# Banded attention beside two routed expert layers: the band's place, the pace of the chains, and the row buffers

## The chip, the cores and the metric

The kernel runs on one core of one Trainium2 chip. The metric is the device time of one execution in microseconds (us). In the text PE is the engine of the matrix products (TensorE), PEld its weight loads, DVE the vector engine, ACT the scalar engine, POOL the GpSimd engine, SP the engine that issues most of the transfers. SBUF is the on-chip memory, PSUM the memory that PE writes its products to.

## The reference

Four batches of 512 rows, each row 128 wide, go through four stages, each followed by a residual sum and a layer norm:

1. attention with 16 heads of width 8, in which row t sees only the rows from t-64 to t+64 (the band): `scores = where(valid, q.k / sqrt(8), -inf)`, softmax over the band, times v, then an output product;
2. a first expert layer: a dense gated block for all rows, and 12 experts of which each row takes two;
3. a state-space layer;
4. a second expert layer: 8 experts of which each row takes two, each with a layer norm of its own.

## The kernel before

**Attention** (`attention`, L858) is one loop over steps. There are eight steps to a batch (`steps = 2 * NT`): four blocks of 128 rows times two halves of the heads. At step g the loop emits, in this order:

- `attention_exp` for step g (L775): PE multiplies q and k for eight heads (the products `pse`, L787, four PSUM banks), ACT takes the exponential into `pt` (L791), POOL zeroes what lies outside the band (L795);
- `attention_max` for step g+9 (L742): the maximum score of each row and head, which is later folded into q so that the exponential does not overflow. For each of four banks (two heads each) PE first writes the band (0 inside, -1e30 outside) into the bank as a product of the identity with a bfloat16 tile (L752), then adds the scores of two heads (`psc`, L758); DVE then takes the maximum of both heads with one `tensor_reduce` per bank (L764);
- `attention_values` for step g-2 (L800): PE multiplies the exponentials with v (L810);
- parts of the next batch's q, k, v (`attention_qk`, `attention_v`);
- `advance(2)` (L906): the next two pieces of every chain that is open.

The loop runs from g = -9 to g = 33. So nine steps hold maxima alone, the steps 0 to 22 hold maxima and exponentials, and the steps 23 to 33 hold no maxima.

**A chain** belongs to a batch b and opens at g = 8b + 9, after that batch's last `attention_values`. It is a Python generator: `attention_out` (L819: scaling by the sums, the product `po` with the output weights, the layer norm) and then `moe0_shared` (L910: the gates, the routing, which ends in eight scatters of rows into a table in DRAM on POOL's queue, L454 and L460, and beside it the dense block). It has 21 `yield`s; each `next` emits one piece, and the 22nd `next` ends it. What is left of the chains after the loop is emitted behind it, one chain after the other, before the expert tiles.

PSUM has a pool of six banks for all of these products (`bank`, L61), handed out in turn: a step of attention takes four for `pse` and four for `psc`.

**The expert layers** (`tiles`, L574) run over 43 and then 39 tiles of 128 rows. In round t, in this order: the loads of tile t+3 (`route_load`, L527: SP issues the rows into a tile `io` and then the expert's weights into `wt`; POOL copies a bias), the transpose of tile t+1 on PE (`pxs`, L548), the up products of tile t with their activations, and the down product of tile t-1, whose result DVE writes into the same `io`; POOL then scatters it from there to DRAM (`ys`, L460). So an `io` buffer is held from the load of its tile until that tile's scatter has been read out. There are six `io` buffers (L534) and four `wt` buffers. In the second layer POOL also adds a bias row into `io` (L1545), copies the bias of tile t+3 (L539) once DVE has used that of tile t-1 (L1563), and DVE takes statistics (L1560 to L1566).

**The order** on each engine is the order in which the Python code emits (`as_written`, L76): every engine runs its instructions in that order, scatters alone may pass one another. Nothing is reordered by a scheduler inside this part.

Of the kernel before, what the change touches and what calls it, by code (L numbers as in the profile page):

```python
# [9 lines left out]
F32 = mybir.dt.float32  # L10
BF16 = mybir.dt.bfloat16
I32 = mybir.dt.int32
AF = mybir.ActivationFunctionType
ALU = mybir.AluOpType
AX = mybir.AxisListType

P = 128
# [3 lines left out]
D = 128  # L21
# [11 lines left out]
NEG = -1.0e30  # L33
# [6 lines left out]
class Kernel:  # L40
# [91 lines left out]
    def consts(self):  # L132
        nc, c = self.nc, self.const

        def t(shape, name):
            return c.tile(shape, F32, tag=name, name=name)

        self.ident = t([P, P], "ident")
        make_identity(nc, self.ident)

        def filled(value, name, shape=(P, 1)):
            x = t(list(shape), name)
            nc.gpsimd.memset(x, value)
            return x

        self.eps5 = filled(1e-5, "eps5")
        self.eps6 = filled(1e-6, "eps6")
        self.half_pi = filled(math.pi / 2, "half_pi")

        self.ident_bf = c.tile([P, P], BF16, tag="ident_bf", name="ident_bf")  # L150
        nc.vector.tensor_copy(self.ident_bf, self.ident)
        self.band = c.tile([P, 256], BF16, tag="band", name="band")
        nc.gpsimd.memset(self.band, 0.0)
        nc.gpsimd.affine_select(
            out=self.band, in_=self.band, compare_op=ALU.is_ge, fill=NEG,
            base=0, pattern=[[1, 256]], channel_multiplier=-1,
        )
        nc.gpsimd.affine_select(
            out=self.band, in_=self.band, compare_op=ALU.is_ge, fill=NEG,
            base=2 * HALF, pattern=[[-1, 256]], channel_multiplier=1,  # L160
        )

        self.rev = t([P, 16], "rev")
        for e in range(16):
            nc.gpsimd.memset(self.rev[:, e : e + 1], float(16 - e))


        self.ones_bf = c.tile([P, P], BF16, tag="ones_bf", name="ones_bf")
        nc.gpsimd.memset(self.ones_bf, 1.0)
        self.before = c.tile([P, P], BF16, tag="before", name="before")  # L170
        nc.gpsimd.affine_select(
            out=self.before, in_=self.ones_bf, compare_op=ALU.is_gt, fill=0.0,
            base=0, pattern=[[1, P]], channel_multiplier=-1,
        )
        self.one_row = filled(1.0, "one_row", (P, 16))
        self.zero = filled(0.0, "zero", (P, ROW))
        number = c.tile([P, 64], I32, tag="number", name="number")
        nc.gpsimd.iota(number, pattern=[[1, 64]], base=0, channel_multiplier=0)
        self.tile_no = t([P, 64], "tile_no")
        nc.vector.tensor_copy(self.tile_no, number)  # L180
        self.first_row = t([P, 16], "first_row")
        nc.vector.tensor_scalar(self.first_row, self.tile_no[:, :16], float(NB * T), None, ALU.mult)

        place = c.tile([P, NB * NT], I32, tag="place", name="place")
        nc.gpsimd.iota(place, pattern=[[2 * P, NB * NT]], base=0, channel_multiplier=2)
        self.place = t([P, NB * NT], "place_f")
        nc.gpsimd.tensor_copy(self.place, place)
        dump = c.tile([P, 48], I32, tag="dump", name="dump")
        nc.gpsimd.iota(dump, pattern=[[P, 48]], base=0, channel_multiplier=1)
        self.dump = t([P, 48], "dump_f")  # L190
        nc.gpsimd.tensor_copy(self.dump, dump)
# [335 lines left out]
    def route_load(self, r, t, up, w, biases):  # L527

        nc = self.nc
        self.route_regs(r, t)  # L530
        reg = r["reg"]
        wt = self.wt.tile([P, 6 * D], F32, tag="wt", name=f"wt_{r['name']}{t}")[:, :w]
        bias = self.wt.tile([P, U1], F32, tag="bias", name=f"bias_{r['name']}{t}")[:, : r["bias"]]
        io = self.wt.tile([P, 3 * D + 4], F32, tag="io", name=f"io_{r['name']}{t}", bufs=6)  # L534
        nc.sync.dma_start(out=io[:, :ROW], in_=r["table"][bass.ds(reg[t, 0], P), :])
        nc.sync.dma_start(
            out=wt, in_=up[bass.ds(reg[t, 1], 1)].rearrange("o p w -> (o p) w")
        )
        nc.gpsimd.tensor_copy(bias, biases[:, bass.ds(reg[t, 3], r["bias"])])  # L539
        return {  # L540
            "wt": wt, "bias": bias, "row": io[:, :ROW], "xs": io[:, :D], "xt": io[:, ROW : ROW + D],
            "ys": io[:, ROW + D : ROW + 2 * D + 1],
        }
# [198 lines left out]
    def attention_max(self, b, u, s):  # L742

        nc = self.nc
        j, odd = divmod(u, 2)
        lo, hi = self.reach(j)
        w, off = hi - lo, lo - (j * P - HALF)
        banks = [
            self.bank(f"psc{b}_{u}_{i}").rearrange("p (c s) -> p c s", c=2)[:, :, :w] for i in range(4)
        ]  # L750
        for pp in banks:
            nc.tensor.matmul(  # L752
                pp, lhsT=self.ident_bf, rhs=self.band[:, None, off : off + w].to_broadcast([P, 2, w]),
                start=True, stop=False,
            )
        for i, pp in enumerate(banks):
            strip = slice(32 * i, 32 * i + 32)
            nc.tensor.matmul(  # L758
                pp, lhsT=s["q"][strip, odd, j * P : (j + 1) * P],
                rhs=s["k"][strip, odd::2, lo:hi], start=False, stop=True,  # L760
            )
        for i, pp in enumerate(banks):
            at = 32 * i + self.MAX_ROW[odd]
            nc.vector.tensor_reduce(self.maxima[b % 2][:, j, at : at + 2], pp, AX.X, ALU.max)  # L764

    def attention_max_end(self, b, s):
        nc = self.nc
# [90 lines left out]
    def attention(self, x, behind):  # L858

        self.attention_consts()
        steps = 2 * NT
        ahead, lag = steps + 1, 2
        state = [{} for _ in range(NB)]
        chains = []

        def chain(b):
            y = yield from self.attention_out(b, state[b])
            yield from behind(b, y)  # L870

        def advance(n):
            for c in list(chains):
                for _ in range(n):
                    if next(c, None) is None:
                        chains.remove(c)
                        break

        for _ in self.attention_qk(0, x[0], state[0]):
            pass  # L880
        self.attention_zeros()
        for g in range(-ahead, NB * steps + lag):
            b, u = divmod(g, steps)
            if 0 <= b < NB:
                self.attention_exp(b, u, state[b])
            b, u = divmod(g + ahead, steps)
            if u == 0 and 0 < b <= NB:
                self.attention_max_end(b - 1, state[b - 1])
            if b < NB:
                self.attention_max(b, u, state[b])  # L890
            b, u = divmod(g - lag, steps)
            if 0 <= b < NB:
                self.attention_values(b, u, state[b])
                if u == steps - 1:
                    chains.append(chain(b))
            if g == -ahead:
                self.attention_weights()
            b, u = divmod(g + ahead + 4, steps)
            if 0 < b < NB and u < 3:
                if u == 0:  # L900
                    state[b]["qk"] = self.attention_qk(b, x[b], state[b])
                next(state[b]["qk"])
            b, u = divmod(g + steps - 3, steps)
            if u == 0 and b < NB:
                self.attention_v(b, state[b])
            advance(2)  # L906
        return (part for c in chains for part in c)


# [788 lines left out]
```

## Time and profile before

| | us |
|---|---|
| median of 5 runs (826.05 to 832.53) | 829.85 |
| the profiled execution, its whole time | 826.89 |
| its span in the profile | 825.2 |

| engine, share of the span busy | |
|---|---|
| PE | 547.3 us, 66% |
| DVE | 426.7 us, 52% |
| POOL | 369.5 us, 45% |
| ACT | 310.0 us, 38% |

By stage, in time from the start of the span: weights arrive and the first maxima wait for them until about 34; maxima alone until 60.7; attention with maxima until about 201; attention without maxima until 264; the rest of the chains until 313; tiles of the first expert layer until 430; the state-space layer until 675; tiles of the second expert layer until about 786; combining and output until 825.

How to read it: a row of a timeline gives the start, the duration, the engine, the line, the operation, what it writes and reads, and how many instructions were merged (x4); in brackets stands how long the engine had been idle before it, and what ended that. A row of waits gives the waiting engine and line, what it waited for, the total, the number of times and the longest. PEclk is the granted clock of TensorE as a share of full speed.

### The profile page before, as it was taken

How to read it: one execution, taken by the hardware profiler on the slowest of the kernel's cores; microseconds unless marked ns; L12 is line 12 of the kernel's file. 1: busy time of each engine (PE TensorE's matmuls, PEld its weight loads, DVE VectorE, ACT ScalarE, POOL GpSimd, SP SyncE). 2: the span in 40 equal slices, each digit the busy share in tenths (PEclk: the TensorE clock that was granted, in tenths of full speed). 3: DMA queues.
4: the chain of work that ended last, by engine and by line, in shares of the span. 5: the costliest groups of instructions: out<-in, count | busy, mean ns of one | idle time of the engine just before them, and what ended most of it. 6: DMA issues, size and time to landing. Idle time of an engine off the chain costs nothing.

```text
span 825.2 us, 12715 instructions
## 1 busy us (share of the span) xinstructions
PE 547.3 (66%) x3912; PEld 383.1 (46%) x3912; DVE 426.7 (52%) x1384; ACT 310.0 (38%) x787; POOL 369.5 (45%) x515
## 2 busy tenths in 40 slices
PE   4389997899859356888863365656766428787700
PEld 1035452454535335887861143433544328676700
DVE  2375573576414243555543587595554335665645
ACT  2014445425644113444432547033131205455503
POOL 8103352274563342444442434366354445666641
PEclk8599997899966677999995758575575558999955
DMA  7999999960000005676747011111110124555431
GB/s 157 206 149 148 149 147 148 151 97 7 8 20 7 19 27 168 205 207 185 211 131 202 0 54 51 38 48 44 45 33 20 33 74 129 144 155 143 130 109 51
DMA packets 93933, 83.58 MB, mean 101 GB/s; under 512 B 8869, under 2 KB 78650, under 8 KB 93866
## 3 DMA queue, kind: packets, MB, share of 16 engines
q1 hardware_dynamic: 88554, 71.85, 43.6%
q0 software_dynamic: 5312, 10.92, 4.4%
q8 instruction: 32, 0.52, 0.3%
q14 instruction: 35, 0.29, 0.1%
HBM read 50.54 MB, written 32.20 MB: 100 GB/s over the span
## 4 chain that ended last, share of the span: by engine, by line
PE 38%; DVE 18%; DMA 13%; issue 11%; ACT 9%; POOL 8%; SPq 2%; POOLq 1%; ACTq 0%; DVEq 0%
DMA io_b<-table_b 4%; PE pse L787 4%; PE psc L758 4%; ACT pt L791 3%; PE pc L810 3%; POOL ys_a L460 3%; PE psc L752 2%; DMA io_a<-table_a 2%; PE py L1398 2%; PE tp_xt L284 2%; PE ph L1550 2%; DVE m L1348 2%; PE ppj L1085 2%; PE py L1394 2%; DVE y L1014 2%
## 5 line engine op out<-in xcount | busy, mean ns | idle before, releaser
L795 POOL TENSOR_SCALAR_AFFINE_SELECT pt<-pt 128x1024 f32<-128x1024 f32 (+1 forms) x64 | 61.6, 985 | 133.8 <-ACT pt L791 130.2
L764 DVE TENSOR_REDUCE maxima<-psc 128x2 f32<-128x384 f32 (+1 forms) x128 | 71.0, 617 | 59.3 <-PE psc L758 53.8
L791 ACT ACTIVATE pt<-pse 128x384 f32<-128x384 f32 (+1 forms) x128 | 59.8, 550 | 74.0 <-PE pse L787 73.9
L460 POOL DMA_INDIRECT ys_a<-io_a,at_a x43 | 42.1, 980 | 59.4 <-DVE at_a L559 52.6
L995 DVE SCALAR_TENSOR_TENSOR act<-pa,bias_a,ge 128x128 f32<-128x128 f32 x129 | 37.3, 345 | 57.7 <-ACT ge L994 35.4
L752 PE MATMUL psc<-band,ident_bf 128*128 128x384 bf16 (+1 forms) x128 | 40.2, 382 | 30.2 <-DVE maxima L764 19.6
L1553 ACT ACTIVATE hid<-ph,bias_b 128x128 f32<-128x128 f32 x156 | 44.6, 369 | 25.2 <-PE ph L1550 17.5
L787 PE MATMUL pse<-q,k 32*128 32x256 f32 (+1 forms) x512 | 48.8, 401 | 0.5 <-ACT pt L791 0.4
L460 POOL DMA_INDIRECT table_b<-r,put x32 | 32.2, 1007 | 33.9 <-DVE e_cnt L447 15.4
L994 ACT ACTIVATE ge<-pg,bias_a 128x128 f32<-128x128 f32 x129 | 38.1, 366 | 21.3 <-DVE at_a L559 7.5
L1550 PE MATMUL ph<-io_b,wt_b 128*128 128x128 f32 x312 | 43.2, 283 | 0.0
L460 POOL DMA_INDIRECT ys_b<-io_b,at_b x39 | 39.1, 1003 | 8.3 <-issue 5.7
L787 PEld LDWEIGHTS pse<-q,k 32*128 32x128 f32 x512 | 35.5, 201 | 14.4 <-issue 8.0
L568 PE MATMUL py_b<-down,hid 128*128 x312 | 42.1, 279 | 0.0
L460 POOL DMA_INDIRECT table_a<-x,put x32 | 32.5, 1016 | 19.9 <-issue 13.8
L1367 POOL TENSOR_TENSOR m<-m,gg 128x512 f32<-128x512 f32 x16 | 26.2, 1661 | 31.2 <-DVE m L1348 31.2
L1550 PEld LDWEIGHTS ph<-io_b,wt_b 128*128 128x128 f32 x312 | 39.5, 198 | 0.0
L568 PEld LDWEIGHTS py_b<-down,hid 128*128 128x128 f32 x312 | 38.7, 195 | 0.2 <-ACT hid L1553 0.2
L292 ACT ACTIVATE rstd<-mv,eps 128x4 f32<-128x4 f32 x16 | 4.7, 297 | 88.3 <-DVE mv L312 79.3
L758 PE MATMUL psc<-k,q 32*128 32x384 f32 (+1 forms) x256 | 37.0, 651 | 0.9 <-ACT k L719 0.9
L986 PE MATMUL pg<-io_a,wt_a 128*128 128x128 f32 x258 | 36.7, 279 | 0.0
L986 PE MATMUL pa<-io_a,wt_a 128*128 128x128 f32 x258 | 36.5, 278 | 0.0
(340 smaller groups left out, 1279.4 us busy)
## 6 DMA issues: line engine op xcount, KB each, us to landing
wt_a<-in_We_dram SPq DMA_DIRECT2D x43, 384.0 KB
table_a<-zero SPq DMA_DIRECT2D x12, 1040.0 KB
wt_b<-in_w_dram SPq DMA_DIRECT2D x39, 256.0 KB
table_b<-zero SPq DMA_DIRECT2D x8, 1040.0 KB
dbc<-rows SPq DMA_DIRECT2D x8, 512.0 KB
io_a<-table_a SPq DMA_DIRECT2D x43, 65.0 KB
io_b<-table_b SPq DMA_DIRECT2D x39, 65.0 KB
down<-in_We_dram SPq DMA_DIRECT2D x12, 192.0 KB
```

The lines of the kernel that those rows point to most:

```text
L460: put = self.nc.gpsimd.indirect_dma_start(out=out, out_offset=bass.IndirectOffsetOnAxis(ap=at, axis=0), in_=x, in_offset=None)
L568: nc.tensor.matmul(py[:, :D], lhsT=hidden[:, c * P : (c + 1) * P], rhs=flat[:, bass.ds(r["reg"][t, 2] + c * D, D)], start=c == 0, stop=c = ...
L752: nc.tensor.matmul(pp, lhsT=self.ident_bf, rhs=self.band[:, None, off : off + w].to_broadcast([P, 2, w]), start=True, stop=False,)
L758: nc.tensor.matmul(pp, lhsT=s["q"][strip, odd, j * P : (j + 1) * P], rhs=s["k"][strip, odd::2, lo:hi], start=False, stop=True,)
L764: nc.vector.tensor_reduce(self.maxima[b % 2][:, j, at : at + 2], pp, AX.X, ALU.max)
L787: nc.tensor.matmul(pp[:, c], lhsT=s["k"][strip, 2 * cp + c, m * P : (m + 1) * P], rhs=s["q"][strip, c, lo:hi], start=True, stop=True, skip ...
L791: nc.scalar.activation(pt[:, 2 * i : 2 * i + 2, :w], pp, AF.Exp)
L795: nc.gpsimd.affine_select(out=x, in_=x, compare_op=ALU.is_ge, fill=0.0, base=HALF if m == 0 and sign > 0 else 0, pattern=[[0, 2 * G], [sig ...
L986: nc.tensor.matmul(p[:, c * P : (c + 1) * P], lhsT=wt[:, at : at + P], rhs=xt, start=True, stop=True,)
L994: nc.scalar.activation(ge[:, cb], pg[:, cb], AF.Gelu, bias=bias[:, 3 + c : 4 + c])
L1550: nc.tensor.matmul(ph[:, cb], lhsT=s["wt"][:, cb], rhs=s["xt"], start=True, stop=True)
L1553: nc.scalar.activation(hid[:, cb], ph[:, cb], AF.Gelu, bias=s["bias"][:, c : c + 1])
```

## The change

Four edits:

- The band is no longer written into PSUM by PE. The four products of L752 in every `attention_max` are gone, and the product of the scores opens and closes its bank alone. The bfloat16 identity and the bfloat16 band are gone; the band is a float32 tile in SBUF.
- In place of one `tensor_reduce` per bank (two heads), DVE gets one `tensor_tensor_reduce` per head: it adds the band to the scores, writes the sum into a scratch tile `in_reach` in SBUF (two buffers), and gives the maximum. In the built program each of these stands as two instructions on DVE: the main one, and a second, 128x1, that writes the maximum out.
- `advance(2)` becomes `advance(3)`.
- `io` has eight buffers where it had six.

```diff
-        self.ident_bf = c.tile([P, P], BF16, tag="ident_bf", name="ident_bf")
-        nc.vector.tensor_copy(self.ident_bf, self.ident)
-        self.band = c.tile([P, 256], BF16, tag="band", name="band")
+        self.band = t([P, 256], "band")
...
-        io = self.wt.tile([P, 3 * D + 4], F32, tag="io", name=f"io_{r['name']}{t}", bufs=6)
+        io = self.wt.tile([P, 3 * D + 4], F32, tag="io", name=f"io_{r['name']}{t}", bufs=8)
...
-        for pp in banks:
-            nc.tensor.matmul(
-                pp, lhsT=self.ident_bf, rhs=self.band[:, None, off : off + w].to_broadcast([P, 2, w]),
-                start=True, stop=False,
-            )
         for i, pp in enumerate(banks):
             strip = slice(32 * i, 32 * i + 32)
             nc.tensor.matmul(
                 pp, lhsT=s["q"][strip, odd, j * P : (j + 1) * P],
-                rhs=s["k"][strip, odd::2, lo:hi], start=False, stop=True,
+                rhs=s["k"][strip, odd::2, lo:hi], start=True, stop=True,
             )
         for i, pp in enumerate(banks):
             at = 32 * i + self.MAX_ROW[odd]
-            nc.vector.tensor_reduce(self.maxima[b % 2][:, j, at : at + 2], pp, AX.X, ALU.max)
+            for c in range(2):
+                in_reach = self.ctx.tile([P, 256], F32, tag="in_reach", name="in_reach")
+                nc.vector.tensor_tensor_reduce(
+                    in_reach[:, :w], pp[:, c], self.band[:, off : off + w], 1.0, NEG, ALU.add, ALU.max,
+                    self.maxima[b % 2][:, j, at + c : at + c + 1],
+                )
...
-            advance(2)
+            advance(3)
```

## Prediction

> **What bounds the kernel now.** I read first the busy time in the stages, then timelines inside them, then the waits of SP. Columns of the first view: stretch, its length, then busy us (and instructions) of PE, PEld, DVE, ACT, POOL, then PEclk, DMA share, GB/s.
>
> ```profile
> 34.00:60.70 26.70, 22.31 (x107) 8.20 (x107) 20.35 (x42) 3.48 (x5) 0.00 (x0) 0.82 1.26 149
> 60.70:108.50 47.80, 46.12 (x431) 23.86 (x429) 26.10 (x50) 22.48 (x46) 18.45 (x20) 1.00 1.27 149
> 108.50:200.00 91.50, 80.88 (x684) 41.26 (x684) 51.48 (x127) 44.40 (x82) 40.22 (x43) 0.93 0.95 115
> 200.00:264.00 64.00, 49.65 (x438) 31.14 (x439) 24.59 (x80) 31.20 (x59) 33.60 (x40) 0.79 0.03 11
> 264.00:313.00 49.00, 24.40 (x100) 15.87 (x98) 19.36 (x66) 8.51 (x14) 18.36 (x24) 0.72 0.06 21
> 313.00:426.00 113.00, 96.20 (x802) 91.92 (x803) 56.28 (x249) 48.75 (x170) 46.97 (x79) 0.97 0.69 200
> 675.00:780.00 105.00, 80.18 (x640) 75.26 (x641) 59.63 (x252) 53.11 (x191) 65.14 (x109) 0.95 0.53 146
> ```
>
> PE bounds attention while there are maxima (96%, then 88% busy; DVE 55%). From 200 to 313 no engine is full: chains run on their latency. The tiles are nearly PE's, with holes. Timeline of DVE and PE in a step without a chain:
>
> ```profile
> 105.58 1.11 PE L752 MATMUL psc<-band,ident_bf 128*128 128x512 bf16 x4
> 106.61 1.14 PE L758 MATMUL psc<-k,q 32*128 32x512 f32 x8
> 107.69 0.86 PE L810 MATMUL pc<-pt,v 128*32 128x192 f32 x16
> 108.47 1.77 PE L787 MATMUL pse<-q,k 32*128 32x256 f32 x16
> ```
> ```profile
> 107.77 2.48 DVE L764 TENSOR_REDUCE maxima<-psc 128x2 f32<-128x512 f32 x4 [2.17 <-PE psc L758]
> ```
>
> The band takes PE about 1.05 us of this step, and DVE sits idle 2.17 us before its four maxima. Four 684 ns reductions end in 2.48 us: one each 0.6 us.
>
> After attention, the last chain's PE work waits for POOL, whose queue first empties the scatters of the chain before:
>
> ```profile
> 274.40 0.97 POOL L460 DMA_INDIRECT table_a<-x,put  x1 [0.31 <-issue]
> 275.68 0.97 POOL L460 DMA_INDIRECT table_a<-x,put  x1 [0.30 <-issue]
> 276.68 1.27 POOL L840 TENSOR_TENSOR sum<-sum,scale 128x512 f32<-128x512 f32 x1
> ```
>
> In the tiles, PE runs one every 2.12 us until the rows are late:
>
> ```profile
> 384.16 0.27 PE L548 MATMUL pxs_a<-ident,io_a 128*128 128x128 f32 x1
> 386.27 0.27 PE L548 MATMUL pxs_a<-ident,io_a 128*128 128x128 f32 x1
> 389.17 0.33 PE L548 MATMUL pxs_a<-ident,io_a 128*128 128x128 f32 x1 [0.61 <-DMA io_a<-table_a]
> ```
>
> and SP's own waits say why they are late: the load waits until a scatter has given its buffer back.
>
> ```profile
> SPq L535 <- DMA ys_a<-io_a,at_a: 30.5, 17, 4.0
> SPq L535 <- DMA ys_b<-io_b,at_b: 30.3, 21, 3.5
> ```
>
> **Price of the new DVE work.** Per head, two instructions. The main one adds an SBUF operand to a PSUM operand and writes SBUF: the row with that shape is L1423 (128x256, 414 ns); 64 elements fewer cost (692-414)/256 x 64 = 70 ns by L850 (512 wide, 692 ns), so 345 ns at 192. Queued work overlaps by 0.07 us (684 ns against 0.62), so 0.345 and 0.275 are the low ends. The second instruction, 128x1, is not in the trace: between 0.06 (a 32x1 memset, L1258, 59 ns) and 0.16 (L559 on 128x1, 159 ns). I take 0.47 (256) and 0.40 (192), mean 0.435 us, nearest to L1423 with a short second part and some overlap. Ends: 0.37 and 0.54 in the mean. A step's eight heads take 3.5 us; its four reductions took about 2.2. So DVE gets 1.3 us more in each of 32 steps, 42 us. PE loses 1.0 us per step, about 34 us in all (128 products; 40.2 us busy by the page, which counts overlap).
>
> [...]
>
> **Part by part.**
>
> 1. Maxima alone (34 to 60.7): DVE is busy 20.35 of 26.7 us. Some 8.5 steps x 1.3 = 11 us more; its idle 6.3 us was mostly PE's band and goes. Sum **+5.5**.
>
> 2. Steps 0 to 8, no chain (47.8 us, 5.3 a step): PE falls to 5.3-1.05 = 4.2; DVE needs 3.5 + 0.6 (k, v, q: 26.1 less 9 x 2.2 = 6.3 us over 9 steps, 0.7 at most) = 4.1 to 4.2. Both full, so some loss between them; six banks for eight tiles a step leave PE no lead. I take 4.65 a step: **-6**.
>
> 3. Steps 9 to 22, with a chain (91.5 us, 6.5 a step): a chain brings DVE about 17 us (layer norm, gates, transposes; rows L828 to L970), at three pieces over eight steps 2.1 a step instead of 17/11 = 1.5. DVE: 3.5 + 0.6 + 2.1 = 6.2. PE: 6.5 - 1.05 + 0.4 (the chain's 13 us over 8 instead of 11 steps) = 5.9, plus stalls, since PE's chain pieces stand behind DVE pieces of the same step, which queue behind eight heads. I take 6.65: **+2**. Six pieces more are then done by step 22 (18 of the second chain's 22 against 12).
>
> 4. Steps 23 to 33 (200 to 264): those six are gone from steps 23 and 24, which took 17 us, 8.5 each; without product pieces some 5.5: -6. The third chain opened while the second's last scatters were queued: PE waited 6.75 us at 232 for POOL's `sum`. With three pieces 22 calls fit into eight steps, so each chain ends before the next opens (the built order on POOL shows it). But POOL's six scatters in a row, 1.28 each, now stand ahead of the next step's selects; two steps of lag cover that. I take -5. Sum **-11**.
>
> 5. Behind the loop: the last chain's `po` began 13.9 us after its `sum` copy (264.1 to 278.0). Its own path is 2.1 (transposes, reciprocals) + 0.6 + 0.7 + 1.3 and hand-overs, 5.8; two scatters may still be ahead, 7.8. **-6**; one more early piece is nothing measurable.
>
> 6. First tiles: an `io` returns 8 us after its down product (386.5 end of `py`, 387.54 scatter, 391.72 next load issued, 394.5 landed by the 2.4 to 3 us loads here). With six buffers three rounds must cover that: 2.7 us a round; the mean is 2.58 (314.65 to 422.88, 42 rounds). With eight, five rounds: 1.6, below PE's 2.12. The next limits: `wt`, four buffers, freed when the up products end, leaving over 6 us for a 384 KB load; and DMA, 69% busy at 2.58, 83% at 2.15. 42 x (2.58-2.15) = 18 us at best; PE's measured holes are 113-96 = 17, of which 4 are the start. I take **-13**.
>
> 7. Second tiles: mean 2.65 (677.4 to 778.0, 38 rounds). Where rows are there, another loop shows: L1560 at 742.87 and 745.11, 2.24 us apart, through DVE's statistics, POOL's L539 and L1545. 38 x (2.65-2.25) = 15; I take **-14**.
>
> The first 34 us, the state-space layer and the end keep their waits (weights landing; L520 on routing). One conversion (1.1 us) at the start goes under those weights.
>
> Sum: 5.5 - 6 + 2 - 11 - 6 - 13 - 14 = -42.5; 826.9 - 42.5 = 784.4. The profiled execution lies 3 us below the median of the five, so I say **786**.
>
> **Rivals.**
>
> - *DVE becomes the bound (slower).* If a head costs what L1414 takes for 128x256 (663 ns) and 0.16 more, 0.82 and at 192 0.75, a step is 6.3 us. Then part 1 is 8.5 x 4.1 - 6 = +29, part 2 (6.3+0.6-5.3) x 9 = +14, part 3 (9.0-6.5) x 14 = +35; less 17 and 27: +34, **861**. For it: most of DVE's idle is already spent in the forecast. Against: L1423 is the same shape with PSUM and takes 414. It decides from 0.64 us a head, where the 42.5 us are used up (256 heads, four fifths exposed). Chance 0.12.
> - *Three pieces stall PE.* In-order waits of chain pieces add 0.9 us to each of 14 steps and the third chain saves nothing: +11 and +10, **807**. For it: PE waited up to 7 us for such pieces with two. Chance 0.14.
> - *The rows come no earlier*, because `wt` or the DMA share binds: tiles give 7 instead of 27, **806**. Against: no PE wait for `wt` is in the trace. Chance 0.13; with the stalls of the rival before, 827, chance 0.03.
> - *Cheap heads*, 0.37: parts 1 to 3 lose 5, 5 and 8 us more, **768**. Chance 0.14.
> - The change does not do quite what it says (two instructions a head, not one); that is priced above.
>
> The forecast keeps 0.44, its own range 772 to 800. The range 762 to 828 leaves out the slower case and a little below. Faster by over 0.5% (about what a measurement of this kernel can tell from no change): 0.44 + 0.14 + 0.13 + 0.14 = 0.85, less a little for mixtures, 0.84; within it 0.04; slower 0.12.
>
> **What would show it.** No L752; the main instruction near 0.41 and 0.35 us, the second under 0.16; DVE over 80% busy from 60 to 190; PE's waits for `psc` banks now ended by DVE; POOL's L840 of the last batch no longer behind scatters; `pxs` 2.15 and 2.25 us apart with no wait for rows, SP's waits on `ys` gone. A main instruction over 0.6 us, or DVE idle behind PE's chain pieces, would make the forecast wrong.

## The result and the profile after

The changed kernel takes 826.48 us (median of 52 runs, 817.52 to 831.59) against 829.0 us (94 runs, 820.44 to 837.79): a ratio of 0.9966, 95% interval 0.9953 to 0.9979. That is faster by 0.34%, inside the half per cent that the prediction set as the bound of "no change". The prediction was 786 us. The time lies just within its range (762 to 828 us), but by no merit of its reasoning: near the upper end it had only a case in which the rows come no earlier (827 us, chance 0.03), and here they do. The profiled execution took 824.23 us, its span 822.5 (before 826.89 and 825.2).

Set side by side, the two traces show a gain and a loss that nearly cancel. The marks are the first start of an operation (for a step, of its exponentials on ACT):

| stretch | before, us | after, us | difference | predicted |
|---|---|---|---|---|
| to the first exponential (maxima alone) | 61.4 | 60.4 | -1.0 | +5.5 |
| step 0 to step 10, no chain | 48.3 | 45.1 | -3.2 | -6 |
| step 10 to step 23, a chain in nearly every step | 93.2 | 133.3 | **+40.1** | +2 |
| step 23 to the last step's exponentials | 51.5 | 56.2 | +4.7 | -11 |
| from there to the first `pxs_a` | 60.2 | 51.0 | -9.2 | -6 |
| first to last `pxs_a` | 108.2 | 91.2 | -17.0 | -13 |
| first to last `pxs_b` | 100.6 | 84.0 | -16.6 | -14 |

One execution is not the kernel: a second trace of the changed kernel (run 5 below, the fastest of its twelve, 814.53 us) has 125.0 us from step 10 to step 23. So some 8 of the 40 us change from one execution to the next.

The busy time of the changed kernel in the same stages (attention runs to 295 us now, so the stretches end later); columns as before: stretch, length, busy us and instructions of PE, PEld, DVE, ACT, POOL, then PEclk, DMA share, GB/s.

```profile
34.00:60.70 26.70, 22.83 (x88) 13.18 (x86) 23.28 (x131) 3.78 (x6) 0.00 (x0) 0.69 1.33 146
60.70:107.00 46.30, 45.87 (x402) 28.43 (x401) 32.11 (x178) 24.24 (x51) 19.93 (x21) 0.93 1.26 149
107.00:190.00 83.00, 69.20 (x431) 39.06 (x428) 37.44 (x185) 29.53 (x55) 28.02 (x32) 0.69 1.04 127
344.00:442.00 98.00, 94.19 (x816) 93.92 (x817) 57.63 (x254) 50.30 (x173) 47.95 (x82) 0.95 0.77 231
```

DVE did not fill up: 37.4 us of 83 from 107 to 190. PE's clock is what changed most there: 0.69, against 0.93 before. A busy share of PE at that clock is long products here, not much work (the 83 us hold 431 products of 0.161 us of busy time each, the 91.5 us of before held 684 of 0.118).

The heads on DVE are cheap. Timeline of DVE in the changed kernel, two heads of width 256:

```profile
102.58 0.08 DVE L759 DVE_READ_ACCUMULATOR2_ANT maxima<- 128x1 f32 x1
102.58 0.42 DVE L759 CUSTOM_DVE_ANT_0 in_reach<-psc,band 128x256 f32<-128x256 f32 x1
102.93 0.08 DVE L759 DVE_READ_ACCUMULATOR2_ANT maxima<- 128x1 f32 x1
102.93 0.42 DVE L759 CUSTOM_DVE_ANT_0 in_reach<-psc,band 128x256 f32<-128x256 f32 x1
```

One head every 0.35 us: the 0.08 us of the second instruction lie under the next head's start.

But PE did not get its 1.05 us a step back. A step without a chain, at a granted clock of 1.00, PE first, then its weight loads (PEld):

```profile
77.12 1.17 PE L785 MATMUL pse<-q,k 32*128 32x256 f32 x16
78.08 2.54 PE L751 MATMUL psc<-k,q 32*128 32x512 f32 x8
80.55 1.07 PE L808 MATMUL pc<-pt,v 128*32 128x256 f32 x16
```
```profile
79.01 0.29 PEld L751 LDWEIGHTS psc<-k,q 32*128 32x128 f32 x2 [0.42 <-ACT pt L789]
79.50 0.29 PEld L751 LDWEIGHTS psc<-k,q 32*128 32x128 f32 x2 [0.20 <-ACT pt L789]
```

The eight instructions of the scores took 1.14 us before and take 2.54 now. The second row of loads says why: the third and fourth bank are still being read by ACT's exponentials of the same step (six banks, eight tiles a step), and come free one by one, 0.5 us apart. Before, the four band products ran in just that time: from 86.55 to 88.03 us they start 0.5 us apart, the last two of them held 0.17 us each by ACT's exponentials.

In a step with a chain, PE stands. The first row is the first chain's `po` before the change, the others are from the changed kernel:

```profile
118.95 1.95 PE L845 MATMUL po<-wo,sum 128*128 128x128 f32 x16
```
```profile
107.65 0.86 PE L808 MATMUL pc<-pt,v 128*32 128x192 f32 x16
111.10 0.49 PE L843 MATMUL po<-wo,sum 128*128 128x128 f32 x2 [2.59 <-POOL sum L838]
111.86 3.31 PE L843 MATMUL po<-wo,sum 128*128 128x128 f32 x14 [0.27 <-DVE sum L838]
...
126.26 2.15 PE L751 MATMUL psc<-k,q 32*128 32x512 f32 x4 [3.23 <-ACT pt L789]
...
149.55 1.01 PE L933 MATMUL tp_gt<-ident,e_g 128*12 128x128 f32 x4 [5.67 <-DVE rh L405]
```

`po` is a chain's product, and stands in PE's queue ahead of the next step's. Before, it waited for nothing. Now it waits 2.6 us for POOL, whose scaling (L838) stands behind two selects (2.14 us together), and then takes 3.8 us at a granted clock of 0.59 (111.0 to 115.2 us). At 149.55 PE has stood 5.67 us for the chain's routing on DVE, ahead of the transposes `tp_gt` of the gates; the first chain before had no such wait. At 126 it is ACT that is late: ahead of the step's exponentials its queue holds the chain's square root and four normalisations (L290, L303), with a table load of 1.28 us on either side, and the normalisations waited for DVE. This wait is not new: before, PE stood 3.20 us for ACT in a like place (131.77 us).

The first tiles went as foreseen. Their products of rows, and SP's waits for buffers (30.5 and 30.3 us before):

```profile
386.35 0.27 PE L546 MATMUL pxs_a<-ident,io_a 128*128 128x128 f32 x1
388.47 0.27 PE L546 MATMUL pxs_a<-ident,io_a 128*128 128x128 f32 x1
```
```profile
SPq L533 <- DMA ys_b<-io_b,at_b: 22.0, 14, 3.8
...
SPq L533 <- DMA ys_a<-io_a,at_a: 12.0, 15, 1.2
```

### The profile page after: what moved, and what is told of

The parts are those of the page before. It is cut to its first block, busy times and chain, and to the rows that moved or that the text cites. A ratio compares the mean times of both kernels' runs of the same rounds, so it can differ in the third digit from the quotient of the medians.

```text
span 822.5 us, 13039 instructions
## 1 busy us (share of the span) xinstructions
PE 561.6 (68%) x3784; PEld 407.6 (50%) x3784; DVE 438.2 (53%) x1767; ACT 310.2 (38%) x788; POOL 368.2 (45%) x515
## 4 chain that ended last, share of the span: by engine, by line
PE 45%; DVE 19%; issue 11%; DMA 9%; ACT 6%; POOL 5%; SPq 3%; another core or an unknown queue 0%; POOLq 0%; ACTq 0%; DVEq 0%
PE psc L751 7%; PE pse L785 5%; DMA io_b<-table_b 4%; PE pc L808 3%; PE pg L984 2%; PE pa L984 2%; PE py L1396 2%; PE ph L1548 2%; DVE m L1346 2%; PE py_a L566 2%; PE py L1392 2%; PE po L843 2%; DVE y L1012 2%; PE py_b L566 1%; PE tp_xt L282 1%
## 5 line engine op out<-in xcount | busy, mean ns | idle before, releaser
L759 DVE CUSTOM_DVE_ANT_0 in_reach<-psc,band 128x192 f32<-128x192 f32 (+1 forms) x256 | 82.6, 386 | 43.1 <-PE psc L751 36.2
L751 PE MATMUL psc<-k,q 32*128 32x512 f32 (+1 forms) x256 | 82.6, 757 | 24.8 <-DVE maxima L759 16.3
L751 PEld LDWEIGHTS psc<-k,q 32*128 32x128 f32 x256 | 39.1, 240 | 48.8 <-issue 22.1
L458 POOL DMA_INDIRECT ys_a<-io_a,at_a x43 | 42.0, 976 | 42.6 <-DVE at_a L557 40.1
L785 PE MATMUL pse<-q,k 32*128 32x256 f32 (+1 forms) x512 | 51.1, 456 | 1.2 <-issue 1.2
L992 ACT ACTIVATE ge<-pg,bias_a 128x128 f32<-128x128 f32 x129 | 38.0, 365 | 21.3 <-DVE at_a L557 16.6
L808 PE MATMUL pc<-pt,v 128*32 128x256 f32 (+1 forms) x512 | 40.8, 441 | 0.7 <-issue 0.6
```

Source lines behind the costliest of these rows:

```text
L458: put = self.nc.gpsimd.indirect_dma_start(out=out, out_offset=bass.IndirectOffsetOnAxis(ap=at, axis=0), in_=x, in_offset=None)
L751: nc.tensor.matmul(pp, lhsT=s["q"][strip, odd, j * P : (j + 1) * P], rhs=s["k"][strip, odd::2, lo:hi], start=True, stop=True,)
L759: nc.vector.tensor_tensor_reduce(in_reach[:, :w], pp[:, c], self.band[:, off : off + w], 1.0, NEG, ALU.add, ALU.max, self.maxima[b % 2][:, ...
L785: nc.tensor.matmul(pp[:, c], lhsT=s["k"][strip, 2 * cp + c, m * P : (m + 1) * P], rhs=s["q"][strip, c, lo:hi], start=True, stop=True, skip ...
L808: nc.tensor.matmul(acc[32 * i : 32 * i + 32, lo:hi], lhsT=s["v"][:, m, 4 * i + 2 * cp + c, :], rhs=pt[:, 2 * i + c, : hi - lo], start=m == ...
L992: nc.scalar.activation(ge[:, cb], pg[:, cb], AF.Gelu, bias=bias[:, 3 + c : 4 + c])
```

## The experiments

**Theory.** The loss is made by the three pieces. A chain's pieces are issued in order with the step's own work, and each one on PE, ACT or POOL holds its whole queue until the piece before it has come through another engine (above: PE for 2.59 us ahead of `po` and 5.67 ahead of `tp_gt`). The time that a chain takes in this way belongs to the chain, not to the step: before, the eleven steps of the first chain (10 to 21) took 83.3 us, after, its eight steps (10 to 18) took 81.7. With three pieces a chain is laid over three steps fewer, and those steps must be done elsewhere. **Rivals:** the DVE heads (chain pieces on DVE stand behind sixteen more instructions); PE's clock; and, for the scores' long products, that the 32-row products no longer run side by side (before, eight of 0.64 us each in 1.14 us) for another reason than banks. Times of kernels that ran together are compared with the kernel before on the same chip; ratios compare across. Runs 1 to 8 ran on one chip, 9 to 11 on a second, 12 on a third.

**1. Eight buffers alone.** `bufs=6` to `bufs=8` for `io` in the kernel before.

> The kernel before with eight io buffers alone; band still by PE, two pieces a step. In the changed kernel the first tiles' products span 91.2 us instead of 108.2 and the second tiles' 84.0 instead of 100.6; if these 33.6 us are the buffers' alone, the time is 829 - 33 = 796 us. Nothing ahead of the first tile should move. Should the tiles have gained from later rows instead (other spacing of the work around them), it would be 805 or more.

Measured: 792.11 us, ratio 0.9575 (0.952 to 0.963). `pxs_a` span 90.1 us, `pxs_b` 84.6, the first `pxs_a` at 315.9 (314.7 before). The buffers are worth the whole 35 us, and the rest of the change has lost them again.

**2. Three pieces, band still by PE.**

```diff
-            advance(2)
+            advance(3)
```

> Eight buffers and three pieces a step, band still by PE. Pieces theory: a chain beside attention takes some 80 us whatever number of pieces a step has (83 us for eleven steps before, 82 for eight in the changed kernel), so three pieces leave three steps a chain uncovered, some 9 to 10 us each time: 796 + 25 to 30 = 821 to 826 us. Rival, the DVE heads: the chains' pieces are late because they queue behind sixteen DVE instructions a step; without those three pieces cost little: 800 us or less.

Measured: 818.72 us, 0.9895 (0.985 to 0.9941): 26.6 us more than the run before, with no DVE head in it. Steps 10 to 18 take 76.1 us. The stall is the one of the changed kernel:

```profile
117.12 3.66 PE L845 MATMUL po<-wo,sum 128*128 128x128 f32 x16 [3.18 <-POOL sum L840]
```

The time is just under the 821 to 826 us that the pieces theory gave, and far from its rival's 800.

From the first exponential to the first `pxs_a` PE does the same products in runs 1 and 2. Run 2 takes 281.9 us there and run 1 254.9: PE stands idle 74.2 us against 53.4, and is busy 207.7 against 201.5, at a granted clock of 0.80 against 0.85. So most of the 27 us are waits, and the rest are longer products.

**3. Band by DVE, eight buffers, two pieces** (the changed kernel with `advance(2)`).

> The changed kernel with two pieces a step: band by DVE, eight buffers. Pieces theory: the first ten steps keep their gain of about 4 us and the chains cover eleven steps again, so 796 - 4 to -12 = 784 to 792 us. Rival, the DVE heads: the loss of 31 us in attention stays for the most part: 815 us or more.

Measured: 789.33 us, 0.9552 (0.9506 to 0.9597). With two pieces the DVE heads are no loss; 2.8 us less than in run 1, with intervals that overlap. In its trace the first `pxs_a` comes at 313.2 instead of 315.9. The rival that the heads make the loss has fallen: this kernel and the changed one differ by the third piece alone, and that piece costs 4.1% (0.9552 against 0.9966), about 34 us. From the first exponential to the first `pxs_a` PE is idle 49.2 us here, and 65.4 and 67.8 us in the two traces of the changed kernel; it is busy 202.6 us here, and 220.2 and 208.7 us there, at a clock of 0.82 against 0.73 and 0.78. The third piece brings 16 to 19 us of waits and 6 to 18 us of longer products.

**4. The same, with the values between exponentials and maxima.**

```diff
             b, u = divmod(g, steps)
             if 0 <= b < NB:
                 self.attention_exp(b, u, state[b])
+            b, u = divmod(g - lag, steps)
+            if 0 <= b < NB:
+                self.attention_values(b, u, state[b])
...
             if b < NB:
                 self.attention_max(b, u, state[b])
-            b, u = divmod(g - lag, steps)
-            if 0 <= b < NB:
-                self.attention_values(b, u, state[b])
```

> As the run before it, with the value products put between the exponentials' products and those of the maxima in each step. Bank theory: in the changed kernel the four products of the maxima take 2.3 to 2.5 us at full clock instead of 1.14, since the third and fourth wait, each by itself, for a bank that ACT's exponential of the same step gives back, a wait that the band products filled. With 0.86 us of value products in that place they take 1.6 us or less, and a step without a chain is 0.5 to 0.8 us shorter: 8 to 15 us less than the run before it. Rival: the 32-row products have lost their side-by-side run for another reason (each opens its bank itself): they still take 2.3 us or more, and the time is within 2 us of the run before it.

Measured: 783.09 us, 0.9466 (0.943 to 0.9502). PE in two steps of this run:

```profile
103.82 0.86 PE L808 MATMUL pc<-pt,v 128*32 128x192 f32 x16
104.61 1.14 PE L751 MATMUL psc<-k,q 32*128 32x512 f32 x8
105.57 2.69 PE L785 MATMUL pse<-q,k 32*128 32x256 f32 x15
```

The scores are back at 1.14 us, so they had lost nothing but their banks: bank theory right. The wait did not vanish. It moved to the exponentials' products, 2.69 us instead of 1.17, which now wait for banks that DVE gives back (their third and fourth pair start at 106.69 and 107.38 us, 0.16 us after DVE's second and fourth head end); so 6 us were gained where 8 to 15 were expected.

**5. The changed kernel again,** as the base of the next three.

> The changed kernel as it is, beside the next three on one chip: 0.9966 of the time before, as measured already; it is the base for the run after it.

Measured: 823.79 us, 0.9974 (0.9949 to 0.9998). The profiled execution took 814.53 us, the fastest of the twelve.

**6. Three pieces, spread over the step.** `advance(1)` after the exponentials, after the maxima and at the end, in place of `advance(3)`.

> The changed kernel with its three pieces a step put one after each of the step's three groups of products (exponentials, maxima, values) instead of all at the step's end. Hand-over theory: a chain takes about 80 us because PE, in order, stands at each piece's product until the piece before it has passed through DVE, POOL or ACT (82 us / 22 pieces = 3.7 us a piece); with 0.9 to 2.4 us of products between two pieces, 1 to 1.5 us a step is covered in 24 steps: 24 to 36 us less than the changed kernel, 790 to 802 us. Rival, the amount of work: three pieces a step simply give DVE and POOL more than a step lasts; where they stand in it matters little: within 5 us of the changed kernel, 821 to 831 us.

Measured: 806.41 us, 0.9756 (0.9686 to 0.9826): 17 us less than run 5, steps 10 to 18 in 65.3 us instead of 75.9. It is the same work with the same number of pieces a step, so their place counts and not only their amount; less was regained than expected. The first `po` still waited 3.4 us for POOL, and all four together 28.1 us, where the two traces of the changed kernel have 19.8 and 20.5.

**7. Two pieces, spread,** one after the values and one at the end, on run 4.

> Eight buffers, band by DVE, value products ahead of those of the maxima, two pieces a step, one after the value products and one at the end. Hand-over theory: a piece's wait is covered by the maxima's products, about 1 us in each of 24 to 33 steps with a chain: 783 - 20 to -30 = 753 to 763 us. Rival, the amount of work: 780 to 786 us.

Measured: 795.68 us, 0.9603 (0.9542 to 0.9663): a miss, 12.6 us more than run 4. In the trace, DVE's heads once wait 10.6 us for the scores: the chain's `pys` products, 7.5 us (0.79 and 1.22 us a group, as long as in the changed kernel at a granted clock of 0.50), now stand on PE between the values and the scores. A piece in the middle of a step holds up the step's own later products. That this is the whole of the 12.6 us was not shown: 2.5 us of it lie in one step ahead of every chain (step 2 to 3, 7.1 us against 4.6); the granted clock from 61 to 110 us was 0.88 here and 0.93 in run 4.

**8. One piece a step, and the rest in turns,** on run 4.

```diff
-            advance(2)
-        return (part for c in chains for part in c)
+            advance(1)
+        def rest():
+            while chains:
+                for c in list(chains):
+                    part = next(c, None)
+                    if part is None:
+                        chains.remove(c)
+                    else:
+                        yield part
+        return rest()
```

> As the run before it, but one piece a step for each chain, and what is left of the chains behind the loop done in turns, one piece of each. Hand-over theory: each piece has a whole step to pass through the other engines, so a step costs little over its products (4.5 to 5 us): 34 steps end near 225 us instead of 252, and 42 pieces in turns take some 75 us: 765 to 778 us. If the chains' pieces do not overlap behind the loop (2.7 us each, one after another), 113 us: 808 us.

Measured: 757.63 us, 0.9158 (0.9098 to 0.9219), below the expectation. The last step's exponentials come at 218.0 us (247.8 in run 4), and the first `pxs_a` at 281.1 (308.3).

**9. One piece, the rest one chain after another.**

> As the run with one piece a step (757.6 us), but what is left of the chains behind the loop is done one chain after another, as in the kernel before. The loop should end as early (218 us there). Hand-over theory: 42 pieces one after another at some 2.7 us each (before: 22 pieces between 254 and 313 us, with nothing beside them) take 113 us instead of 63: about 800 to 808 us. Rival, that the order behind the loop does not matter: 755 to 762 us.

Measured: 777.06 us, 0.9413 (0.9364 to 0.9461), between the two expectations. The loop ends as early (220.7), but the first `pxs_a` comes at 297.9. Beside run 4 this is within the intervals: in the traces one piece a step ends the loop 27.1 us earlier, and the some 40 pieces left, one chain after another, give 16.6 of them back. Of the 22.5 us between the traces of runs 9 and 8 the turns account for 14.0 (77.1 against 63.1 us from the last step's exponentials to the first `pxs_a`); 2.5 lie in a step ahead of every chain (the granted clock from 61 to 110 us was 0.87 here and 0.93 in run 8), and some 4 in a stretch of the state-space layer that no edit touches.

**10. As run 8, with the band by PE and the old order.**

> One piece a step and the rest in turns, eight buffers, but the band by PE and the step's order as before: what the DVE heads are worth where the chains no longer hold PE. If PE's products then set the step, the band's 1.05 us counts in most of 32 steps and the time is 757.6 + 15 to 30 = 773 to 788 us. If banks, not PE, set the step (the wait that moved from the maxima's products to the exponentials', 2.1 to 2.7 us instead of 1.2), the band is nearly free: 757.6 + 0 to 10 = 758 to 768 us.

Measured: 766.17 us, 0.9296 (0.9256 to 0.9337), in the range given for banks, and not PE, setting the step.

**11. The changed kernel with zeros through the PE openers.**

```diff
+        for pp in banks:
+            nc.tensor.matmul(
+                pp, lhsT=self.ident_bf, rhs=self.nil[:, None, off : off + w].to_broadcast([P, 2, w]),
+                start=True, stop=False,
+            )
...
-                rhs=s["k"][strip, odd::2, lo:hi], start=True, stop=True,
+                rhs=s["k"][strip, odd::2, lo:hi], start=False, stop=True,
```

> The changed kernel, with the four PE products that open the banks put back, but with zeros in place of the band; DVE still adds the band. Eight buffers with three pieces a step and the band by PE gave 818.7 us, the changed kernel 823.8 beside its own runs. If the maxima's four products are long (2.3 to 2.5 us) only because of the wait for banks, they return to about 1.14 us and the time moves by no more than 6 us from the changed kernel, since chains set these steps. If fewer PE products lower PE's granted clock (0.83 against 0.68 from 110 to 190 us) and that makes the changed kernel slower than with PE's band: 819 us or less, with the clock near 0.8. If the DVE heads make it slower: 824 to 832 us.

Measured: 830.56 us, 1.0063 (1.0037 to 1.0089), clock 0.87 from 110 to 190 us. PE:

```profile
109.56 1.04 PE L754 MATMUL psc<-nil,ident_bf 128*128 128x512 bf16 x4
110.53 1.14 PE L760 MATMUL psc<-k,q 32*128 32x512 f32 x8
```

The scores take 1.14 us again, behind 1.04 us of openers: together 2.2, against 2.5 without openers. Steps 0 to 10 took 51.1 us against 46.7 in run 5: at most 0.44 us a step for the openers, not 1.05, and 2.4 of the 4.4 us lie in the first step alone. The better clock (0.68 and 0.77 in the two traces of the changed kernel, same stretch) brought no better time: steps 10 to 18 took 75.4 us, in the changed kernel 81.7 and 75.9. So a clock lowered by fewer products on PE does not explain the changed kernel's loss. The run lies 7 to 8 us above the changed kernel, outside the 6 us that the bank theory allowed and in the range that was given to the DVE heads. About 3 to 5 us of that are a stretch that no edit touches (last `pso` to last `pl` in the state-space layer: 12.2 us; 9.5 and 7.2 in the changed kernel; 10.7 and 11.5 in the other two runs on this chip), so the total does not decide for the heads.

**12. The changed kernel with one piece and turns, nothing else.**

> The changed kernel with one piece a step and the rest in turns, nothing else (the step's order as in the changed kernel: the maxima's products ahead of the values). It splits the 8.5 us between the run with one piece, turns, DVE and the new order (757.6 us, 0.9158 of before) and the one with PE's band and the old order (766.2 us, 0.9296). If the order gives here what it gave with two pieces, 6 us, 0.923 and 763 to 764 us, so the DVE heads alone are worth some 3 us again. If the DVE heads are worth all of it, 757 to 759 us.

Measured: 754.38 us, 0.9212 (0.9182 to 0.9242) beside its own runs of the kernel before. Against run 10 the DVE heads are worth 0.8%, some 7 us, and the intervals are apart; from the first exponential to the first `pxs_a` the traces differ by as much (218.7 against 225.9 us). Whether the order is worth its 6 us again is not decided: the ratio is 0.0054 above that of run 8, the intervals overlap, and the first `pxs_a` (278.9) is not later. In its trace the first chain's `po` waits for nothing and takes 1.95 us instead of 3.8:

```profile
124.47 1.07 PE L808 MATMUL pc<-pt,v 128*32 128x256 f32 x16
125.47 1.13 PE L710 MATMUL pk<-xt,w_WkT 128*128 128x512 f32 x2
126.43 1.95 PE L843 MATMUL po<-wo,sum 128*128 128x128 f32 x16
```

POOL had scaled its part of `po`'s input from 121.1 to 122.8 us, one step ahead. Steps 10 to 18 take 40.6 us, against 60.3 before and 81.7 in the changed kernel. Runs 8 and 12 beat both kernels by some 8%. Against the kernel before, half of that is the eight buffers (run 1).

## Why the prediction was wrong, point by point

- **Steps 9 to 22 (+2): the step that failed.** "I take 6.65" a step; the thirteen from step 10 to step 23 took 10.3 (9.6 in run 5). The sum gave a chain's share of DVE's and PE's *work* to each step (6.2 and 5.9 us) and left less than 1 us for "stalls", worked out from nothing. But PE, in order, waits at the chain's products: the steps of the first chain took 75 to 84 us at three and at two pieces a step (65 and 90 us where three and two were spread). So the third piece took away three steps that a chain had covered, and it cost 26.6 us in run 2 against run 1 and some 34 in the changed kernel against run 3. The rival *Three pieces stall PE* had the mechanism; it put 0.9 us on each of 14 steps (12.6 us, where it wrote 11) and came to 807 us; its 21 us for the stalls fall short of both differences.
- **Steps 0 to 8 (-6): half.** 3.2 us came. The forecast wrote "six banks for eight tiles a step leave PE no lead" and still counted 0.65 us a step; what it left out is that the band products ran in a time in which the scores' banks were not free (run 4).
- **Maxima alone (+5.5): sign wrong, small.** It went 1.0 us down; a head costs less than priced. The traces of the other runs spread from 58.5 to 62.7 us here, so 1 us tells little.
- **Steps 23 to 33 (-11): wrong.** +4.7. The six pieces done earlier had taken their time in the steps before, and these steps still took 7.0 us each where 5.5 were forecast for those without maxima.
- **Behind the loop (-6): direction right (-9.2), reason wrong.** Run 2, with PE's band, has 51.2 us here too, and run 3 60.2: it is the third piece. By the count of calls 20 are left behind the loop where 25 were before (the last chain has one more than the others). Of the last chain's scaling it was said that two scatters might still be ahead of it. In the changed kernel six stand in a row ahead of it, and `po` waits 9.95 us for POOL where it waited 8.10. The last of the six and rows of what follows:

```profile
304.93 0.96 POOL L458 DMA_INDIRECT table_a<-x,put  x1 [0.30 <-issue]
307.03 0.62 POOL L831 COPY wide<-inv 128x512 f32<-128x512 f32 x1
308.54 1.70 POOL L838 TENSOR_TENSOR sum<-sum,scale 128x512 f32<-128x512 f32 x1 [0.89 <-DVE scale L834]
```

- **First tiles (-13) and second tiles (-14): right.** -17.0 and -16.6. In the first tiles by the mechanism named: two more buffers cover the 8 us of an `io`'s return, PE's 2.12 us a tile becomes the limit, and PE waits once more for rows, 1.8 us. In the second tiles the mean is 2.21 us, as forecast (2.25), but not by the loop named: many tiles are 1.9 to 2.0 us apart, and eleven times PE still waits for rows, 7.5 us in all. SP's waits shrank instead of going.
- **Price of a head (0.47 and 0.40): too high.** 0.35 and 0.28 us, the low ends. Heads start 0.07 us before the one ahead of them has ended, and the 83 ns of the accumulator's read are hidden under the next head's start. The main instruction, with one source in PSUM, takes 419 ns, as L1423 without a maximum (414).
- **DVE over 80% busy from 60 to 190 us: wrong** (54%), because steps grew longer; the waits for `psc` banks end with ACT's exponentials, not with DVE.

What stays open: with three pieces the band by DVE comes out slower than by PE (0.9966 and 0.9974 against 0.9895), while with one piece it is faster. Two profiled executions of the changed kernel differ by as much in attention (278 and 287 us from the first exponential product to the first `pxs_a`; the run with three pieces and PE's band has 283), so the runs here do not tell why. Nor is it shown which wait of a chain sets its pace: `po` behind POOL, the routing on DVE and the normalisations on ACT all appear.

## What to carry to other kernels

When a latency-bound chain is laid in pieces beside a loop on in-order queues, price its hand-overs, not its work alone: each exposed one holds a whole queue (here PE for 2.59 and 5.67 us), and at two or three pieces a step their sum belonged to the chain. One piece a step over more steps, with several chains open at once and what is left done in turns, hid most of it (run 12 beside the changed kernel: 7.6%; beside run 3, two pieces: 3.6%); a third piece a step lost 4.1%. And before counting an operation's time as saved, look what else ends in that time: here the next product's banks.

## What was not expected of the hardware

At a lower granted clock the same products took longer. Here is the first of the same four pairs of products of a chain in two executions of the same changed kernel, first the one shown above, then run 5:

```profile
168.29 0.79 PE L961 MATMUL pys<-be,gt 13*128 13x128 f32 x2
169.01 1.22 PE L963 MATMUL pys<-w_Ws,act_s 128*128 128x128 f32 x4
```
```profile
170.56 0.48 PE L961 MATMUL pys<-be,gt 13*128 13x128 f32 x2
170.97 0.71 PE L963 MATMUL pys<-w_Ws,act_s 128*128 128x128 f32 x4
```

The granted clock was 0.50 from 170 to 180 us in the first and 1.00 in the second: 7.5 against 4.2 us for all four pairs. The first chain's `po` ran at a granted clock of 0.59 (3.8 us, where it took 1.95 before at 1.00) behind 2.6 us of waiting. The clock also tells the two executions apart: from the first exponential to the first `pxs_a` they took 285.6 and 276.5 us, with PE idle 65.4 and 67.8 us, but busy 220.2 and 208.7, at a granted clock of 0.73 and 0.78. With the run of zeros, whose clock was better (0.87 from 110 to 190 us) and whose time was not (830.56 us), the clock does not look like the cause of the stalls. Whether the stalls lower it is not shown: no run here sets the clock by itself.
